# A sparse attention block on one core: the first tile's slot groups, the late neighbour lists and a late mean factor

## The chip, the cores and the metric

The kernel runs on 1 core of a Trainium2 chip, in one launch. The metric is the device time in microseconds (us). Time before: a median of 1792.07 us over 3 runs, from 1788.15 to 1799.92 us.

## The reference

One layer of graph attention over 4096 nodes with rows of 512 floats, float32 throughout, followed by a feed-forward block and a layer norm:

```
hs, ht = layer_norm(x), layer_norm(h_target)           # 4096 x 512
q, k, v = ht @ Wq + bq, hs @ Wk + bk, hs @ Wv + bv     # 8 heads of 64
logits = q.k / 8, -1e30 where adj == 0                 # 4096 x 4096, int32 adjacency
ctx = softmax(logits) @ v
ht = layer_norm(ht + ctx @ Wo + bo)
y = ht + gelu(ht @ W1) @ W2                            # W1 512 x 2048, W2 2048 x 512
out = layer_norm(x + y)
```

The adjacency is sparse: it is symmetric, has its diagonal set, and about 16 of 4096 entries of a row are ones (at most 39 here). So the kernel never forms the 4096 x 4096 logits: it makes lists of neighbours and gathers their key and value rows.

## The kernel before

**Two parts, written out by hand.** In part one, three generators are woven: `projections()` computes key and value rows of all nodes and writes them to a table `kvd` in device memory; `prepare()` makes the neighbour lists of tiles 0 to 15 (`NA` = 16, the early lists), sorts their rows by degree and starts the first query rows; `fill()` makes the lists of the next 7 tiles (`FILL` = 7). In part two, four generators are woven: `att` (attention), the chain of `feed(g)` (feed-forward), `other_lists()` (the last 9 tiles of lists, then `sort(1)` of tiles 16 to 31), and `weights()` (the second half of W1 and W2).

`_weave` keeps a due time for each generator and always runs the one that is due first; what a generator yields is added to its due time. These due times are units of the plan, not microseconds. Attention takes 60 units (`UNIT`) for a group of two tiles, and so does `feed`. `other_lists` starts at `WAIT` = 100 units and multiplies what `edges` yields by 2.2; a tile of late lists yields 12 in all, so that it takes 26.4 units. A stream that yields `None` sleeps until another one has run.

**Lists (`edges`, L716).** A tile of 128 adjacency rows comes in four quarters of 512 KB (`quarter`, L708, issued on SP). Those of tiles below `RINGED` = 22 go into rows 0 to 7 of a buffer `ring`; the later ones into two rows called `wide`. ScalarE takes the sign (L733), VectorE multiplies by positions (L740) and takes maxima (L742), and after four quarters decodes them (L749 to L766). Quarters are asked for ahead of the one in work, also by the last early tile for those of the first late tile.

**Sort (`sort`, L808).** Degrees are counted into bins with two matmuls and scans, ranks are computed (L864 to L867), and 16 indirect DMAs on GpSimd (POOL) scatter the records (L871), each 3.0 units after the last in part two. The records of part two must be there when attention asks for those of tile 16.

**Attention.** Tiles hold rows of like degree; tile i has a cap of neighbour slots. The order of caps by group is [11], [13, 14], [15, 15], [16, 17], [17, 18], [19, 19], [20, 22], [23, 24], [39, 12], [38, 13], [24, 14] and so on to [18]: 17 groups, 603 slots. Slots are worked in groups of `S` = 3 with what remains of the cap at the end. POOL gathers one slot (128 rows of 4 KB) with each L985. VectorE multiplies keys by the query (L1239) and sums per head (L1244), ScalarE takes the exponential (L1248, L1257) and scales the third slot (L1223), VectorE scales the first two (L1200) and adds some (L1204), TensorE adds the transposed values into `cps` (L1211). Gathers run 4 slot groups ahead (`AHEAD`) in `ring`, which has 17 rows for them at first and 20 once the lists are done; `place` says which rows.

**`finish` (L1096)** spreads the rest of a tile over later steps of attention (`advance()` runs every open tail twice per slot group): output projection (L1132), the copy of `h` (L1137), statistics (L697), variance plus epsilon (`n_ve`, L680), the power -1/2 on POOL (`power`, L687), the mean factor on VectorE (`negmean`, L692), the normalization on ScalarE (L1150), the transposes (L1159). Only then is `h2T` there, for which `feed(g)` sleeps.

**`feed(g)`** makes the hidden layer (L1344), its gelu (L1347) and the output (L1353); `end` (L1294) then spreads the last layer norm over the steps of the next `feed`: sum (L1300), squares (L1305), `n_ve` (L1309), power (L687), mean factor (L1314), normalization (L1317), scatter of the rows on POOL (L1321).

Of the kernel before, what the change touches and what calls it, by code (L numbers as in the profile page):

```python
# [443 lines left out]
def adj_resnorm_kernel(  # L444
# [38 lines left out]
    NT = N // P  # L483
# [4 lines left out]
    NQ = 4  # L488
# [7 lines left out]
    TILES = [t for g in groups for t in g]  # L496
# [4 lines left out]
    NA, NBT = len(CAPS_A), len(CAPS_B)  # L501
    PARTS = ((0, len(CAPS_A)), (len(CAPS_A), len(CAPS_B)))
    S = 3
# [29 lines left out]
    with tc.tile_pool(name="keep", bufs=1) as keep:  # L533
# [17 lines left out]
        with ExitStack() as late:  # L551
# [152 lines left out]
            adjs = []  # L704
            DEEP = 8
            FILL = 7
            RINGED = NA + FILL - 1
# [12 lines left out]
            def edges(i):  # L720

                part = 1 if i >= NA else 0
                rec = Rs[part][:, i - PARTS[part][0], :]
                cand = lp.tile([P, SEG, 8], U16, name="cand", bufs=2)
                for h in range(NQ):
                    n = i * NQ + h
                    while len(adjs) < min(n + 2, NT * NQ):
                        adjs.append(quarter(*divmod(len(adjs), NQ)))
                    a, adjs[n] = adjs[n], None

                    sg = turn_of("signs", signs)
                    with behind(newest if i >= NA else []):
                        nc.scalar.activation(sg, a, AF.Sign, accum_out=dpart[:, i, h:h + 1])  # L733
                    ahead = min(n + DEEP - 1, n + 3 + n // 2)
                    while len(adjs) < min(max(n + 3, min(ahead, RINGED * NQ)), NT * NQ):
                        adjs.append(quarter(*divmod(len(adjs), NQ)))
                    yield 0.0 if i < NA else 0.7 if i < NA + FILL else 1.0
                    wd = sg.bitcast(U16)
                    with behind(logits):
                        nc.vector.tensor_tensor(wd, wd, lio, ALU.mult)  # L740
                    for s, (w0, w1) in enumerate(SEGS):
                        maxima[:] = [nc.vector.max(cand[:, h * SQ + s, :], wd[:, w0:w1]).ins]  # L742
                    if h == 1:
                        keep_rest()
                    if h % 2 and moms:
                        moments(moms.pop(0))
                    yield 1.8 if i < NA else 0.7 if i < NA + FILL else 1.0
                dec = dec_w
                nc.vector.tensor_single_scalar(dec[:, 0], cand, 255, op=ALU.bitwise_and)  # L749
                nc.vector.tensor_single_scalar(dec[:, 1], cand, 8, op=ALU.logical_shift_right)  # L750
                gid = lp.tile([P, 2 * SEG, 8], F32, name="gid")
                dec = dec.rearrange("p b s e -> p (b s) e")
                off = segoff.rearrange("p b q s -> p (b q s)")
                nc.vector.scalar_tensor_tensor(gid, dec, 0.0,
                                               off.unsqueeze(2).to_broadcast([P, 2 * SEG, 8]),
                                               op0=ALU.is_gt, op1=ALU.mult)
                nc.vector.scalar_tensor_tensor(gid, dec, 2.0, gid, op0=ALU.mult, op1=ALU.add)
                flat = gid.rearrange("p s e -> p (s e)")
                for r in range(RE // 8):
                    top = rec[:, E0 + r * 8:E0 + (r + 1) * 8]  # L760
                    nc.vector.max(top, flat)
                    if r + 1 < RE // 8:
                        nc.vector.match_replace(flat, top, flat, 0.0)
                held.append((rest_d[i * P:(i + 1) * P, :], flat))
                has = lp.tile([P, MAXE], F32, name="ehas")
                nc.vector.tensor_scalar(has[:, :RE], rec[:, E0:E0 + RE], 0.0, 0.0, op0=ALU.is_gt,  # L766
                                        op1=ALU.add, accum_out=cnt[:, i:i + 1])
                yield 2.4 if NA <= i < NA + FILL else 4.0
# [45 lines left out]
            def sort(part):  # L814

                i0, n = PARTS[part]
# [52 lines left out]
                for i in range(n):  # L869
# [5 lines left out]

                    tc.declare_no_dep(ins.ins, group=f"scatter{part}", reason="other rows")
                    tc.add_to_no_dep_group(f"scatter{part}", ins.ins)
                    yield 3.0 if part else 1.3
                done.add(part)


# [119 lines left out]
            def front(i, idle=0):  # L1001
# [28 lines left out]
                for kc in range(KC):  # L1030
# [10 lines left out]

            SG = [(i, j0, min(S, cap - j0)) for i, (_, cap) in enumerate(TILES)
                  for j0 in range(0, cap, S)]
            kvs, rests, fronts = {}, {}, {}
            place = [11]
            for i, _, n in SG:
# [48 lines left out]
            def finish(i, p, cps, group, hs, mv):  # L1095
# [48 lines left out]
                ve = shifted(sp, mv[:, :nh, :], nh, "n2")  # L1144
                yield
                rs = power(sp, mv[:, :nh, :], nh, "n2", ve)
                yield
                nm = negmean(sp, mv[:, :nh, :], rs, nh, "n2")
                for j, h in enumerate(hs):
                    nc.scalar.activation(h, h, AF.Identity, bias=nm[:, j:j + 1], scale=rs[:, j:j + 1])  # L1150
# [144 lines left out]
            def end(group, xs, po):  # L1295
# [14 lines left out]
                yield  # L1310
                rs = power(sp, None, nt, "n3", ve)
                yield
                nm = sp.tile([P, nt], F32, name="n3_nm")
                nc.vector.tensor_mul(nm, sm[:, :nt, 0], rs)  # L1314
                yield
# [81 lines left out]
                for g in gens:  # L1397
                    yield from g

            WAIT = 100.0  # L1400
            AHEAD = 4
            ADDS = 11
            HEAVY = 30
# [67 lines left out]
                        load_quarter(pool, q + 2, nc.scalar)  # L1471

            def other_lists():
                for cost in ed:
                    yield 2.2 * cost
                keep_rest()
                yield from sort(1)

# [37 lines left out]
```

## Time and profile before

| | |
|---|---|
| median of 3 runs | 1792.07 us |
| the profiled execution | 1783.65 us, of which the span (first to last instruction) 1781.9 us |
| TensorE busy | 1666.0 us, 93% of the span |
| VectorE busy | 1425.0 us, 80% |
| ScalarE busy | 1240.4 us, 70% |
| POOL busy | 1018.9 us, 57% |
| mean granted TensorE clock | 0.971 |
| bytes moved | 461.0 MB, 259 GB/s over the span |

The profile gives each engine's busy time as an average over stages that have different limits, so that the views by time window and by waits matter more. A busy TensorE is not TensorE at its peak. On POOL the 0.3 us between two indirect DMAs are not counted as busy. The first list of part two is worked at 382.55 us of the span, its last at 708 us, the 16 scatters from 768.22 to 851.57 us.

### The profile page before, as it was taken

The page shows a single profiled execution, that of the slowest core. Times are in us where ns is not written, and L with a number is a line of the kernel's source. Part 1 is how long each engine was busy: PE and PEld are TensorE (multiplying, and loading weights), DVE is VectorE, ACT ScalarE, POOL GpSimd, SP SyncE. Part 2 cuts the span into 40 slices and gives each one's busy share as a digit, 9 for nine tenths or more (in the row PEclk, how much of TensorE's full clock was granted, in tenths as well). Part 3 has the DMA queues.
Part 4 walks back from the last instruction along what each step waited for, and adds up shares of the span by engine and source line. Part 5 has one row for each costly group of instructions (what it writes and reads, how often), then busy time and mean ns, then how long its engine had stood idle before and what let it go on. Part 6 is the DMA issues. An engine that isn't in the chain of part 4 may idle for free. (4 is left out here: it accounts for less than half of the span.)

```text
span 1781.9 us, 22463 instructions
## 1 busy us (share of the span) xinstructions
PE 1666.0 (93%) x6850; PEld 1078.9 (61%) x6850; DVE 1425.0 (80%) x2449; ACT 1240.4 (70%) x3133; POOL 1018.9 (57%) x822
## 2 busy tenths in 40 slices
PE   7999994889999999997989999999999999999997
PEld 3444443656666776665657667666666666666665
DVE  6887787868788989996989898989897888988500
ACT  5876673648777888675777877787776777877511
POOL 1000146655557566778886787777677767764101
PEclk9999997899999999998999999999999999999998
DMA  9999988877778797867888788877667777675000
GB/s 353 383 388 367 344 272 324 318 249 270 250 241 308 273 322 268 271 204 232 285 298 284 274 282 294 295 259 260 234 218 269 249 235 239 233 260 194 21 4 26
DMA packets 141610, 461.00 MB, mean 259 GB/s; under 512 B 18036, under 2 KB 23048, under 8 KB 141480
## 3 DMA queue, kind: packets, MB, share of 16 engines
q0 software_dynamic: 96272, 342.33, 56.7%
q1 hardware_dynamic: 37392, 94.06, 14.9%
q10 hardware_dynamic: 7816, 23.08, 3.3%
q8 instruction: 57, 0.93, 0.2%
q14 instruction: 73, 0.60, 0.1%
HBM read 430.61 MB, written 28.79 MB: 258 GB/s over the span
## 5 line engine op out<-in xcount | busy, mean ns | idle before, releaser
L985 POOL DMA_INDIRECT kv<-kvd,rec x603 | 795.4, 1319 | 335.4 <-issue 118.5
L1344 PE MATMUL pf<-h2T,w 128*128 128x256 f32 (+1 forms) x2176 | 474.5, 372 | 4.5 <-ACT h2T L1163 4.5
L1353 PE MATMUL po<-w,gt 128*128 128x512 f32 x1024 | 463.7, 594 | 0.0
L1344 PEld LDWEIGHTS pf<-h2T,w 128*128 128x128 f32 x2176 | 393.0, 193 | 74.3 <-issue 20.3
L1239 DVE TENSOR_TENSOR kv<-kv,tq 128x1536 f32<-128x1536 f32 (+2 forms) x211 | 351.1, 1675 | 55.6 <-DMA kv<-kvd,rec 52.0
L1223 ACT ACTIVATE kv<-kv,pa 128x64 f32<-128x64 f32 x1520 | 390.9, 336 | 4.4
L1244 DVE TENSOR_REDUCE lg<-kv 128x24 f32<-128x1536 f32 (+2 forms) x211 | 350.0, 1667 | 0.6
L1353 PEld LDWEIGHTS po<-w,gt 128*128 128x128 f32 x1024 | 187.6, 191 | 194.5 <-issue 193.1
L1211 PEld LDWEIGHTS cps<-ident,kv 128*128 128x128 f32 x1828 | 217.6, 144 | 121.5 <-issue 41.8
L1211 PE MATMUL cps<-ident,kv 128*128 128x128 f32 x1828 | 244.1, 280 | 50.1 <-DVE kv L1200 32.1
L1200 DVE TENSOR_TENSOR kv<-kv,p 128x1024 f32<-128x1024 f32 (+1 forms) x211 | 251.1, 1192 | 25.8 <-ACT p L1248 24.4
L687 POOL TENSOR_TENSOR n_rs<-n_ve,mhalf 128x2 f32<-128x2 f32 (+2 forms) x51 | 53.4, 1047 | 327.4 <-DVE n_ve L680 133.0
L733 ACT ACTIVATE kv<-kv 128x1024 uint8<-128x1024 int32 x128 | 134.4, 1052 | 53.4 <-DMA kv<-in_adj_dram 21.8
L1347 ACT ACTIVATE gt<-pf 128x512 f32<-128x512 f32 x128 | 76.4, 597 | 100.9 <-PE pf L1344 97.4
L1347 ACT ACT_TABLE_LOAD x110 | 141.1, 1283 | 1.8
L1132 PE MATMUL t<-wo,rb 128*128 128x512 f32 x256 | 121.0, 615 | 8.1 <-DVE rb L1122 8.1
L947 PE MATMUL pq<-wv,h2T 128*128 128x512 f32 x256 | 117.0, 600 | 3.3 <-DVE rbc L662 2.4
L947 PE MATMUL pq<-wk,h2T 128*128 128x512 f32 x256 | 119.1, 608 | 1.0 <-DVE h2T L928 1.0
L1031 PE MATMUL t<-wq,tq 128*128 128x512 f32 x256 | 116.8, 600 | 1.3 <-ACT tq L1024 1.3
L742 DVE MAX8 cand<-kv 128x8 uint16<-128x171 uint16 (+1 forms) x384 | 108.2, 324 | 1.2
L1248 ACT ACTIVATE p<-lg 128x24 f32<-128x24 f32 (+2 forms) x179 | 38.9, 218 | 75.3 <-DVE lg L1244 73.9
L947 PEld LDWEIGHTS pq<-wv,h2T 128*128 128x128 f32 x256 | 48.9, 193 | 66.8 <-issue 57.5
(163 smaller groups left out, 1586.0 us busy)
## 6 DMA issues: line engine op xcount, KB each, us to landing
kv<-in_adj_dram SPq DMA_DIRECT2D x128, 512.0 KB, 7.3
kvd<-tq ACTq DMA_DIRECT2D x23, 512.0 KB, 6.9
kv<-kvd,rec POOLq DMA_INDIRECT x603, 6.0
kv<-in_L_gnn_h_target_dram SPq DMA_DIRECT2D x32, 256.0 KB, 6.3
kv<-in_x_dram SPq DMA_DIRECT2D x15, 512.0 KB, 8.5
kvd<-kv ACTq DMA_DIRECT2D x9, 512.0 KB, 6.5
w<-in_L_gnn_W_dram SPq DMA_DIRECT2D x4, 1024.0 KB, 8.2
w<-in_L_gnn_W_dram ACTq DMA_DIRECT2D x4, 1024.0 KB, 14.1
```

What stands on the lines that cost most here:

```text
L733: nc.scalar.activation(sg, a, AF.Sign, accum_out=dpart[:, i, h:h + 1])
L947: nc.tensor.matmul(pkv, hT[:, kc, j * P:(j + 1) * P], w[:, kc, :], start=kc == 0, stop=kc == KC - 1)
L985: issues[:] = [nc.gpsimd.indirect_dma_start(out=dst, out_offset=None, in_=table[:, :], in_offset=bass.IndirectOffsetOnAxis(ap=idx, axis=0) ...
L1132: nc.tensor.matmul(pa, ct[:, c, :], wo[:, c, :], start=False, stop=c == KC - 1, skip_group_check=True)
L1200: nc.vector.tensor_tensor(v4, v4, p[:, j0:j0 + m, :].unsqueeze(3) .to_broadcast([P, m, H, HD]), ALU.mult)
L1211: nc.tensor.matmul(cps[:, c, :], kv[:, j, D + c * P:D + (c + 1) * P], ident, is_transpose=True, start=j0 + j == 0 and c == 0, stop=j0 + n ...
L1223: newest[:] = [nc.scalar.mul(v, v, pa[:, hd:hd + 1]).ins]
L1239: nc.vector.tensor_tensor(kv[:, :n, :D], kv[:, :n, :D], tq[:, :D].unsqueeze(1).to_broadcast([P, n, D]), ALU.mult)
L1244: logits[:] = [nc.vector.tensor_reduce(lg[:, :n, :], kv[:, :n, :D].rearrange("p j (h d) -> p j h d", h=H), AX.X, ALU.add).ins]
L1344: nc.tensor.matmul(pf[:, k, :], w1[(f0 + k) // KC][:, kc, (f0 + k) % KC * P:((f0 + k) % KC + 1) * P], h2T[:, kc, :w], start=kc == 0, stop= ...
L1347: nc.scalar.activation(gt, pf, AF.Gelu_apprx_tanh)
L1353: nc.tensor.matmul(po[j], gt[:, k, j * P:(j + 1) * P], w2[(f0 + k) // KC][:, (f0 + k) % KC, :], start=False, stop=f0 + k == FC - 1, skip_g ...
```

## The change

Six edits. The slot groups of tile 0 (11 slots) become 2, 3, 3, 3 instead of 3, 3, 3, 2. `edges` asks for no quarter beyond tile 22 while the early tiles run; `other_lists` asks for two itself and waits 6 units. `other_lists` starts at 134 units instead of 100 and multiplies by 1.6 (`PACE`) instead of 2.2. The scatters of `sort(1)` stand 4.5 units apart instead of 3.0. In `finish`, for tiles from 16 on, four yields instead of one stand between the power on POOL and the mean factor. In `end` two yields stand there instead of one.

```
@@ edges
+                    top = (NA + FILL if i < NA + FILL else NT) * NQ
-                    while len(adjs) < min(n + 2, NT * NQ):
+                    while len(adjs) < min(n + 2, top):
...
-                    while len(adjs) < min(max(n + 3, min(ahead, RINGED * NQ)), NT * NQ):
+                    while len(adjs) < min(max(n + 3, min(ahead, RINGED * NQ)), top):
@@ sort
-                    yield 3.0 if part else 1.3
+                    yield 4.5 if part else 1.3
@@ slot groups
             SG = [(i, j0, min(S, cap - j0)) for i, (_, cap) in enumerate(TILES)
                   for j0 in range(0, cap, S)]
+            short = TILES[0][1] % S
+            if short:
+                SG[:-(-TILES[0][1] // S)] = [(0, 0, short)] + [(0, j0, S) for j0 in
+                                                              range(short, TILES[0][1], S)]
@@ finish
                 rs = power(sp, mv[:, :nh, :], nh, "n2", ve)
-                yield
+                for _ in range(1 if i < NA else 4):
+                    yield
                 nm = negmean(sp, mv[:, :nh, :], rs, nh, "n2")
@@ end
                 rs = power(sp, None, nt, "n3", ve)
                 yield
+                yield
                 nm = sp.tile([P, nt], F32, name="n3_nm")
@@ constants
-            WAIT = 100.0
+            WAIT = 134.0
+            PACE = 1.6
@@ other_lists
+                for _ in range(2):
+                    adjs.append(quarter(*divmod(len(adjs), NQ)))
+                yield 6.0
                 for cost in ed:
-                    yield 2.2 * cost
+                    yield PACE * cost
                 keep_rest()
                 yield from sort(1)
```

## The prediction

> **What bounds the kernel now.** I read the busy times first, then windows of 10 and 50 us, then the timeline of TensorE for its gaps, and at each gap what the waiting engine waited for.
>
> ```profile
> PE 1666.0 (93%) x6850; PEld 1078.9 (61%) x6850; DVE 1425.0 (80%) x2449; ACT 1240.4 (70%) x3133; POOL 1018.9 (57%) x822
> ```
>
> TensorE (PE) is full nearly everywhere, and from 1650 us it works alone on the last feed-forward groups. The end comes when its work is done, so the kernel gains what PE stops losing. Its gaps of 0.8 us and more sum to 93.4 us: 14.2 in part one, 29.4 from 271 to 336 us, where part two fills, 49.8 later. The timeline shows the large later ones, by the instruction that ends each, with the idle time in brackets:
>
> ```profile
> 400.78 2.82 PE L1211 MATMUL cps<-ident,kv 128*128 128x128 f32 x12 [5.43 <-DVE kv L1200]
> 834.75 1.97 PE L1211 MATMUL cps<-ident,kv 128*128 128x128 f32 x8 [12.46 <-DVE kv L1204]
> 933.37 2.82 PE L1211 MATMUL cps<-ident,kv 128*128 128x128 f32 x12 [6.56 <-DVE kv L1200]
> 1257.78 1.11 PE L1159 MATMUL t<-ident,h 128*128 128x128 f32 x4 [4.06 <-DVE tq L1036]
> 1347.11 1.12 PE L1159 MATMUL t<-ident,h 128*128 128x128 f32 x4 [4.19 <-DVE tq L1036]
> ```
>
> Three causes. First, at 389 to 405 us: the feed-forward of group 0 is over, that of group 1 waits for its `h2T`, and just then the late lists start (first L733 at 382.55). Second, at 834 and 933: VectorE (DVE) waits for gathers, because POOL is full. In the windows the fifth pair is POOL; with 0.3 us between two instructions, 68.63 + 52 x 0.3 = 84.2 of 84 us:
>
> ```profile
> 768.00:852.00 84.00, 70.80 (x316) 50.15 (x315) 68.72 (x72) 58.25 (x161) 68.63 (x52) 0.92 0.69 217
> 852.00:950.00 98.00, 90.17 (x399) 61.36 (x398) 86.79 (x94) 71.48 (x204) 77.88 (x64) 0.97 0.87 297
> 823.03 1.76 DVE L1239 TENSOR_TENSOR kv<-kv,tq 128x1536 f32<-128x1536 f32 x1 [10.63 <-DMA kv<-kvd,rec]
> ```
>
> Third, at 1257 and 1347: DVE stands before the mean factor L692, since the power on POOL is queued behind gathers; behind L692 on DVE wait the values (L1204, L1200) and the query (L1036).
>
> ```profile
> 1246.75 0.16 DVE L692 SCALAR_TENSOR_TENSOR n_nm<-mv,n_rs 128x2 f32<-128x2 f32 x1 [4.10 <-POOL n_rs L687]
> 1339.84 0.16 DVE L692 SCALAR_TENSOR_TENSOR n_nm<-mv,n_rs 128x2 f32<-128x2 f32 x1 [7.84 <-POOL n_rs L687]
> ```
>
> **What the Trainium skill says.** "TensorE: Matmul & The Clock Gate", Part 1: an idle window of about 3.4 us halves the PE clock, and a busy one restores it. The trace agrees: after the gap at 834.75, 8 transposes take 1.97 us against 1.04 before it, and 16 L1344 take 5.18 against 3.62, so 2.5 us more are lost; after 400.78 it is 2.9 in the same way. The same page, Architectural detail, says that ScalarE, VectorE and POOL queues are strictly first in, first out; L692 above, with ready work behind it, agrees. "DMA: Bandwidth & Descriptors", Anatomy of one DMA, prices a POOL transfer at 2.0 us plus bytes at 436 GB/s, 3.2 us for 512 KB; here the median gather lands after 6.0 us, and I use the trace.
>
> **The change, part by part.** Sums stand against the profiled execution, 1783.65 us (span 1781.9), which is 8.4 below the median. A unit of the plan is about 1.49 us: from 100 units (382.55 us) to the first scatter at 358 units (768.22 us) pass 386 us.
>
> *Head: no late quarters early, and 2 slots first.* The first gather starts at 274.19:
>
> ```profile
> 274.19 0.97 POOL L985 DMA_INDIRECT kv<-kvd,rec  x1 [17.46 <-DMA rest_d<-gid]
> 282.32 1.76 DVE L1239 TENSOR_TENSOR kv<-kv,tq 128x1536 f32<-128x1536 f32 x1 [2.19 <-DMA kv<-kvd,rec]
> ```
>
> It needs the last `kvd` write, issued by ScalarE at 267.58. On SP two quarters, 1 MB, were issued at 265.42; at the 390 GB/s of this stage they hold the DMA engines for 2.7 us ahead of that write. Without them the first gather is up to 2.5 us earlier. The first L1239 waits for three gathers; with two it has its data one issue, 1.25 us, earlier. The sum of 3.7 is capped by the query: L1036 ends at 280.13, so L1239 moves at most from 282.32 to 280.13, by 2.2 us. Multiplications and reductions of the 11 slots are the same sum; a last group of three puts the 2.0 us of L1223 near the tile's end. The rows of `ring` begin 11, 13, 0, 3, 6 instead of 11, 14, 0, 3, 5, and for the next seven slot groups a row is reused after 5 groups instead of 6, so POOL may wait for the PE of the step just before. Bounds: 4 gained, 3 lost. I take 2 gained.
>
> *Late lists at 134 + 6 units instead of 100.* That is 40 x 1.49 = 60 us later, at about 442 us, past group 1. The gaps at 393.82, 400.78 and 405.19 are 1.98 + 5.43 + 1.59 = 9.0 us, with the clock 11.9. In that stretch DVE did 4.9 us of list work (four L740, twelve L742, first decodes) and waited 3.1 us for gathers beside four quarters. So `h2T` comes up to 8 us sooner; I take 6.5, as a boundary of groups isn't free of gaps even then. Upper end 12, lower end 0.
>
> *The same lists at 1.6 instead of 2.2.* Per tile DVE does four times (0.41 + 3 x 0.325) plus decodes of 3.2, some 8.7 us. In 26.4 units (39 us) that was 22% of DVE, in 19.2 units (28.6 us) it is 30%. From 500 to 750 us DVE was 90% busy (224.7 of 250), so it comes to 98% while the lists last; ScalarE (four times 1.24 us a tile) gets 5 points more on 82%. PE was full there (five windows miss 3.4 us of 250), and little slack remains at the boundaries of groups 2 to 4. No trace shows this load. Nothing lost at best; with attention's demand a few points higher in groups 4 and 5, up to 12 us. I take 4 lost, what one more gap with its cold clock costs.
>
> *Scatters 4.5 units apart.* `sort` begins at 134 + 6 + 9 x 12 x 1.6 = 312.8 units instead of 337.6; scatters run from 332.8 to 404.8 instead of 357.6 to 405.6. The end, which tile 16 waits for, stays. In the old stretch POOL loses 1.3 us per scatter every 5.2 us (25%), now about every 7 (18%). But no work leaves POOL, which never pauses from 768 to 958: what the stretch gains is the (357.6 - 332.8) / 4.5 = 5.5 scatters moved ahead of it, 7 us, and only as far as POOL was idle there (5.2 us beyond the 0.3s from 700 to 766). I take 5 gained, of the 19 of both gaps. Upper end 15, if evenly spaced gathers end the 12.46 us gap with its clock; lower end 0.
>
> *Mean factor three steps later from tile 16.* Waits before L692 go: 4.10, 7.84, 3.66, 5.30, 4.82 us (groups 10 to 14), 25.7 of DVE. In PE only two gaps answer to them, 4.06 + 4.19 = 8.25, and their clock, by the windows some 3: 11 gained. What is late instead is `h2T`, by three `advance()`, 1.5 slot groups. Each `feed` starts with its `h2T`, so once, near group 9, PE has 1.5 slot groups with no feed-forward: a slot group then takes DVE's 4.5 to 5 us, of which PE fills some 2: 4.5 lost. Net 6.5 gained; ends 12 gained and 3 lost.
>
> *One more yield in `end`.* L1314 waited 5.2 us in five places, three of them in the tail where PE alone works. The scatter of rows comes one step later and holds two `xt` buffers, which the next group asks for half a feed later. I take 0, from 2 gained to 2 lost.
>
> Sum: -2 - 6.5 + 4 - 5 - 6.5 = -16; with a share of the gap of 2.65 us at 1067 (same cause as 1257) -18. 1783.65 - 18 = 1765.7; from the median, 1792.07 - 18 = 1774.
>
> **The rivals.** *Gaps only trade places (0 to -8, about 1788).* A full PE in 412 to 750 us speaks for it: POOL is the pacemaker to 958, and an earlier start meets the same queue. Against it: the head and the gap at 400 lie where PE alone was starved, so they shift all that follows. *More goes than I count (-35, 1757).* If even spacing ends both POOL gaps (19 us and 5 of clock) with the L692 gaps, the sum is -16 - 19 = -35. For it: the gap at 834 is one wait of 10.63 us. Against: POOL's total work. *Slower: the denser lists overload DVE.* If the lists' 30% meets an attention that wants over 75% of DVE, as 99.5% in the window 700 to 750 hints, groups 3 to 5 become DVE-bound: if both together ask for 112 to 118% of the 9 x 28.6 = 257 us, PE starves for 31 to 46 us, less the 18 gained elsewhere: +13 to +28, or 1812. It decides from 107% on, where the excess eats the 18.
>
> **How the numbers follow.** My forecast, -8 to -28, gets 0.47; trading 0.19; more 0.17; slower 0.17. About 1% (18 us) is what a measurement of this kernel can tell from no change, and it halves my own case: faster 0.17 + 0.27 = 0.44; most of the slower case, 0.14, is over 1%; within 1% is the rest, 0.42. The likeliest time is 1774. Range 1752 to 1802: from -40 to +10, which leaves out most of the slower case and the end of the third.
>
> **What would show it.** Right: no list before 430 us, the gaps at 393 to 405 down to 3 us or less, first L1239 near 280, scatters from about 730 with POOL still without a pause to 950, L692 in groups 10 to 14 with waits under 1 us, and one new gap of PE of 3 to 5 us near 1160. Wrong: DVE at 98% and PE under 95% between 450 and 720; a gap over 10 us left at 830; `h2T` transposes that start new gaps at each boundary from group 9 on.

## The result, and the profile after

The changed kernel takes 1792.91 us in the median, the kernel before it 1789.51 us beside it: a ratio of 1.0022, 95% interval 1.0008 to 1.0036. The change costs some 4 us; the forecast was a gain of 18. (The ratio is not the quotient of the two medians, which is 1.0019. Here and below, microseconds that a version gains or costs are worked out from its ratio.)

The profiled execution of the changed kernel took 1796.3 us (span 1794.6), that of before 1783.65. This difference of 12.7 us isn't the size of the change: the first profile is at the low end of its kernel's runs (1782.41 to 1799.92), the second in the upper half of its own (1787.98 to 1802.88). Below, durations of waits are read from the profiles and the sizes of effects from the ratios.

Line numbers are those of each version's own file. In the changed kernel L1239 has become L1245, L1244 L1250, L1200 L1206, L1204 L1210, L1211 L1217, L1163 L1169, L1344 L1351, L1353 L1360 and L985 L986; L687 and L692 have kept their numbers. First, busy time by engine, and TensorE's gaps (in brackets the idle time ahead of the instruction and what ended it):

```profile
PE 1669.4 (93%) x6850; PEld 1077.6 (60%) x6850; DVE 1422.6 (79%) x2449; ACT 1232.2 (69%) x3127; POOL 1020.9 (57%) x822
```

```profile
404.91 0.47 PE L1217 MATMUL cps<-ident,kv 128*128 128x128 f32 x1 [4.52 <-DVE kv L1206]
663.65 1.11 PE L1022 MATMUL t<-ident,tq 128*128 128x128 f32 x4 [4.72 <-ACT rb L1124]
666.99 6.48 PE L1360 MATMUL po<-w,gt 128*128 128x512 f32 x8 [2.23 <-ACT gt L1354]
793.58 0.69 PE L1217 MATMUL cps<-ident,kv 128*128 128x128 f32 x2 [5.19 <-DVE kv L1210]
847.43 1.97 PE L1217 MATMUL cps<-ident,kv 128*128 128x128 f32 x8 [4.40 <-DVE kv L1210]
945.70 2.82 PE L1217 MATMUL cps<-ident,kv 128*128 128x128 f32 x12 [5.84 <-DVE kv L1206]
1091.26 4.21 PE L1351 MATMUL pf<-h2T,w 128*128 128x256 f32 x9 [6.13 <-ACT h2T L1169]
```

The gap of 12.46 us at 834 has become several of 3 to 5 us, the one at 1257 has gone, and those at 400 and 933 have stayed. New are 663 and 667, and 1091, where the feed-forward of a group waits for its `h2T`; in place of the gap at 1347 another such wait, of 3.03 us, stands at 1360. The new gap at 663 begins on POOL: a gather of `xt` waits for an earlier scatter into the output to land, the gathers of slots stand behind it in POOL's queue, and DVE waits for those. Timelines of POOL and of DVE:

```profile
646.99 0.97 POOL L986 DMA_INDIRECT xt<-in_x_dram,tags  x1 [7.16 <-DMA out_dram<-xt,tags]
```

```profile
658.61 1.76 DVE L1245 TENSOR_TENSOR kv<-kv,tq 128x1536 f32<-128x1536 f32 x1 [9.09 <-DMA kv<-kvd,rec]
```

The mean factor should have stopped waiting in groups 10 to 14. On DVE's timeline it stands in groups 10 to 12 like this ("issue": the profile shows no releaser):

```profile
1256.50 0.14 DVE L692 SCALAR_TENSOR_TENSOR n_nm<-mv,n_rs 128x2 f32<-128x2 f32 x1
1347.02 0.16 DVE L692 SCALAR_TENSOR_TENSOR n_nm<-mv,n_rs 128x2 f32<-128x2 f32 x1 [6.63 <-issue]
1431.77 0.16 DVE L692 SCALAR_TENSOR_TENSOR n_nm<-mv,n_rs 128x2 f32<-128x2 f32 x1 [7.36 <-POOL n_rs L687]
```

The wait of group 10 went, that of group 12 grew from 3.66 to 7.36. In groups 8 to 15 they sum to 26.6 us, against 26.9 before. The reason is in the order of instructions that the compiler emits. A yield sets only when the program, as it is traced, reaches an instruction; the place on the engine is the compiler's choice, and here it hardly follows the yields. DVE instructions between `n_ve` (L680) and L692, groups 9 to 15:

```
before            1  1  2  2  4  4  1
changed kernel    3  3  2  2  4  4  4
```

In groups 11 to 14 the two kernels have the same instructions there. What the three yields did move is `h2T`, and with it the start of each feed-forward.

The windows of the stretch in which POOL was full, and one of the stretch in which the lists are denser (busy us of PE, PEld, DVE, ACT, POOL, then granted clock, DMA share and GB/s):

```profile
500.00:700.00 200.00, 190.56 (x860) 132.26 (x859) 171.14 (x323) 163.61 (x399) 116.74 (x96) 0.97 0.79 277
768.00:852.00 84.00, 71.03 (x293) 48.96 (x292) 67.70 (x76) 52.94 (x140) 65.22 (x56) 0.93 0.78 253
852.00:950.00 98.00, 90.69 (x392) 61.63 (x392) 86.95 (x95) 73.16 (x203) 79.81 (x61) 0.96 0.83 281
```

From 768 to 852 TensorE has 71.03 us of work, as before (70.80): the long gap was cut into short ones and nothing was won. From 500 to 700 it has 190.56 instead of 197.62, with DVE at 171.14 us, no higher than before (174.96). So what was lost there wasn't DVE's capacity.

The late `h2T` shows at the end of the kernel. These are the last transposes of values and the last matmuls, first in the kernel before, then in the changed one:

```profile
1671.90 0.60 PE L1211 MATMUL cps<-ident,kv 128*128 128x128 f32 x4
1763.18 7.03 PE L1353 MATMUL po<-w,gt 128*128 128x512 f32 x16
```

```profile
1672.66 1.47 PE L1217 MATMUL cps<-ident,kv 128*128 128x128 f32 x12
1775.14 7.03 PE L1360 MATMUL po<-w,gt 128*128 128x512 f32 x16
```

From the end of the former to the end of the latter pass 97.7 us before and 108.0 us after. To the scatter of the last rows, which ends the work, it is 102.9 and 113.2 us; below, this time is called the tail.

### The profile page after: what moved, and what is told of

It reads as the page before. It is cut to its first block, busy times and chain, and to the rows that moved or that the text cites. A ratio compares the mean times of both kernels' runs of the same rounds, so it can differ in the third digit from the quotient of the medians.

```text
span 1794.6 us, 22449 instructions
## 1 busy us (share of the span) xinstructions
PE 1669.4 (93%) x6850; PEld 1077.6 (60%) x6850; DVE 1422.6 (79%) x2449; ACT 1232.2 (69%) x3127; POOL 1020.9 (57%) x822
## 5 line engine op out<-in xcount | busy, mean ns | idle before, releaser
L986 POOL DMA_INDIRECT kv<-kvd,rec x603 | 802.5, 1331 | 319.8 <-issue 128.8
L1351 PE MATMUL pf<-h2T,w 128*128 128x256 f32 (+1 forms) x2176 | 475.9, 372 | 13.0 <-ACT h2T L1169 11.5
L1360 PE MATMUL po<-w,gt 128*128 128x512 f32 x1024 | 465.2, 596 | 6.5 <-ACT gt L1354 6.5
L1351 PEld LDWEIGHTS pf<-h2T,w 128*128 128x128 f32 x2176 | 392.7, 193 | 81.1 <-issue 21.0
L1245 DVE TENSOR_TENSOR kv<-kv,tq 128x1536 f32<-128x1536 f32 (+2 forms) x211 | 351.3, 1675 | 57.9 <-DMA kv<-kvd,rec 52.5
L1250 DVE TENSOR_REDUCE lg<-kv 128x24 f32<-128x1536 f32 (+2 forms) x211 | 350.1, 1666 | 0.9 <-DVE R L762 0.2
L1360 PEld LDWEIGHTS po<-w,gt 128*128 128x128 f32 x1024 | 188.3, 191 | 200.7 <-issue 191.9
L1217 PE MATMUL cps<-ident,kv 128*128 128x128 f32 x1828 | 246.6, 280 | 48.0 <-DVE kv L1206 31.0
L1217 PEld LDWEIGHTS cps<-ident,kv 128*128 128x128 f32 x1828 | 217.2, 144 | 122.3 <-issue 40.4
L1206 DVE TENSOR_TENSOR kv<-kv,p 128x1024 f32<-128x1024 f32 (+1 forms) x211 | 251.3, 1192 | 18.7 <-ACT p L1254 13.8
L687 POOL TENSOR_TENSOR n_rs<-n_ve,mhalf 128x2 f32<-128x2 f32 (+2 forms) x51 | 46.1, 903 | 329.6 <-DVE n_ve L680 163.2
```

The costliest lines, as they stand in the source:

```text
L986: issues[:] = [nc.gpsimd.indirect_dma_start(out=dst, out_offset=None, in_=table[:, :], in_offset=bass.IndirectOffsetOnAxis(ap=idx, axis=0) ...
L1206: nc.vector.tensor_tensor(v4, v4, p[:, j0:j0 + m, :].unsqueeze(3) .to_broadcast([P, m, H, HD]), ALU.mult)
L1217: nc.tensor.matmul(cps[:, c, :], kv[:, j, D + c * P:D + (c + 1) * P], ident, is_transpose=True, start=j0 + j == 0 and c == 0, stop=j0 + n ...
L1245: nc.vector.tensor_tensor(kv[:, :n, :D], kv[:, :n, :D], tq[:, :D].unsqueeze(1).to_broadcast([P, n, D]), ALU.mult)
L1250: logits[:] = [nc.vector.tensor_reduce(lg[:, :n, :], kv[:, :n, :D].rearrange("p j (h d) -> p j h d", h=H), AX.X, ALU.add).ins]
L1351: nc.tensor.matmul(pf[:, k, :], w1[(f0 + k) // KC][:, kc, (f0 + k) % KC * P:((f0 + k) % KC + 1) * P], h2T[:, kc, :w], start=kc == 0, stop= ...
```

## The experiments

All ratios are against the kernel before, run beside the version on the same chip, with 95% intervals; a version has 2 to 22 runs. They were made on six chips, on which the kernel before had medians from 1784.9 to 1793.3 us, so only ratios are compared.

**One part at a time.** The short first slot group alone:

```
+            short = TILES[0][1] % S
+            if short:
+                SG[:-(-TILES[0][1] // S)] = [(0, 0, short)] + ...
```

> The kernel before with tile 0's slot groups as 2, 3, 3, 3 alone. Theory A (the head as in the prediction): the first multiplication waits for two gathers instead of three, 1 to 2 us gained. Rival (the query is what the first multiplication waits for next, and the last group of three costs it back): within 1 us, and DVE's first reduction chain ends no earlier.

Measured: 0.9969 (0.9956 to 0.9983), 5.5 us less. This part gains more than the 2 us that the prediction gave it.

The lists' part, `WAIT` 134, `PACE` 1.6 and scatters 4.5 units apart (without the edit of `edges` and the 6 units of waiting, which were not run by themselves):

> The kernel before with the late lists at 134 units and 1.6, and the scatters 4.5 apart, nothing else. Theory A (the prediction): 7 us gained at the boundary at 400 us and in the POOL stretch, net of the denser lists. Rival B (the denser lists take it back): 2 to 8 us slower, with new gaps of TensorE between 450 and 720 us. Rival C (gaps only trade places): within 2 us.

Measured: 1.0023 (1.0008 to 1.0039), 4 us more, in the range of rival B. TensorE's idle time (the brackets of its timeline, summed) rose by 9.5 us between 345 and 720 us (24.7 against 15.2) and fell by 4.6 between 720 and 860. The gap at the start of group 1 is there with no list near it:

```profile
399.06 1.53 PE L1211 MATMUL cps<-ident,kv 128*128 128x128 f32 x12 [2.04 <-DVE kv L1200]
406.14 2.25 PE L1159 MATMUL t<-ident,h 128*128 128x128 f32 x8 [5.55 <-ACT h L1150]
```

The mean factor alone (`for _ in range(1 if i < NA else 4): yield` ahead of `negmean`):

> The kernel before with four yields instead of one ahead of the mean factor from tile 16 on, nothing else. The order of VectorE's instructions that the compiler made has L692 one to three places behind n_ve in groups 9 to 14, as before, so the yields hardly move it. Theory D (the edit does not reach the instruction stream): the waits before L692 stay at 20 us or more in sum and the time is within 2 us. Theory A (the prediction): waits under 1 us each, 6 us faster.

Measured: 1.0072 (1.0044 to 1.0101), 13 us more. The waits before L692 sum to 25.1 us in groups 8 to 15. A new gap of 4.06 us at 1090 waits for `h2T`, and the tail is 113.2 us instead of 102.9: in the order of instructions, 246 matmuls follow the last transposes of values instead of 226. (A profile counts more: a product of two f32 tiles stands there twice, 16 records for the 8 of one step of L1344.)

The same yields, with the mean factor also bound to a place on DVE behind the newest logits:

```
+                with behind(logits if i >= NA else []):
                     nm = negmean(sp, mv[:, :nh, :], rs, nh, "n2")
```

> The kernel before with the four yields and the mean factor made to stand on VectorE behind the newest reduction of logits, from tile 16 on, so that it really is two slot groups later (8 to 16 instructions between n_ve and L692 in groups 9 to 14). Theory A: L692 waits under 3 us in sum, and the two gaps of TensorE at 1257 and 1347 us go, 6 to 11 us faster. Rival (h2T comes later, so each feed-forward starts later): new gaps of TensorE at the boundaries of groups 9 to 14, 0 to 10 us slower.

Measured: 1.0025 (1.0012 to 1.0038). Here the waits before L692 are gone (0.0 us in groups 8 to 15), but from 1000 to 1650 us TensorE is idle for 15.9 us, as before (16.6), and the tail stays at 113.2 us. The waits were removed together with a late `h2T`, and nothing came of it.

The density alone (`2.2 * cost` to `1.6 * cost`, start at 100 as before):

> The kernel before with only the density of the late lists changed, 1.6 instead of 2.2 units. Theory A (the density is what costs, as predicted): 3 to 6 us slower, 1.002 to 1.003, with TensorE's idle time between 345 and 720 us up by 4 to 9 us and DVE at 95% or more there. Theory B (the density is hidden, and the loss of the lists' part comes from moving the lists to where groups 3 to 5 are, with their scatters closer to the gathers): within 2 us of before.

Measured: 0.9997 (0.9975 to 1.0019). The ratio shows no cost of the density, though the profile has 21.1 us of idle TensorE from 345 to 720.

**The changed kernel without its mean edit and without the yield in `end`.**

> The changed kernel with the mean factor's three yields and the extra yield in end taken back; the short first slot group, the lists past group 1, their density and the scatters stay. Theory A (the mean edit costs: the feed-forward of every group starts 1.5 slot groups later, and the work that TensorE does alone at the end grows by 7.8 us): 4 to 9 us faster than the changed kernel, so 0.996 to 0.999 of the kernel before; from the h2T copy of group 16 to the end 71.8 us instead of 79.6; the gap of 6 us near 1091 us gone. Theory B (parts simply add): slots -5.5 and lists +4.1 give -1.4 us, 0.9992. Theory C (the loss lies in lists and scatters): as the changed kernel, 1.002.

Measured: 1.0007 (0.9992 to 1.0022). Slots and lists cancel each other. In this company the mean edit and the yield in `end` cost 0.15% together, 2.7 us, which the intervals don't tell from nothing; alone the mean edit cost 13.

**Which engine is the bound?** Three kernels leave work out. These three, and later the one with the reciprocal, also leave out the jump to the general path that the kernel takes for unusual inputs. The scatters of part two leave POOL:

```
+                    if part:
+                        ins = nc.sync.dma_start(recs_d[part][i * P:(i + 1) * P, :], R[:, i, :])
```

> The kernel before with the 16 scatters of part two left out of POOL: their rows go out in natural order from SP, so the neighbour lists of part two are not sorted into their tiles. Theory A (the gap at 834 us comes from POOL's total work, of which the scatters are 16 x 1.3 = 21 us): the gap of 12.5 us and the one of 6.6 us at 933 go, some 15 us off the total, 0.992. Theory B (gaps trade places, since other engines are full too): under 6 us off the total, 0.997 or more, with TensorE's idle time coming back after 860 us.

Measured: 0.9995 (0.9974 to 1.0015). With none of the 16 scatters on POOL, the gap before L1204 (here L1210) is still there with 7.63 us, and at 933 one of 1.45 us is left:

```profile
841.18 1.97 PE L1217 MATMUL cps<-ident,kv 128*128 128x128 f32 x8 [7.63 <-DVE kv L1210]
```

The total hasn't moved, but it doesn't measure the scatters alone. After all work, at the very end, an instruction of POOL of the kind DRAIN takes 8.3 us, where it takes 0.97 us in the kernel before and in each of the other versions. These are its three at that place, first in this version, then in the kernel before (ns, minimum, median and maximum):

```profile
L1517 POOLq DRAIN  x3: 44/107/8322, 1786.0 to 1794.8; - x3
```

```profile
L1511 POOLq DRAIN  x3: 44/107/972, 1780.1 to 1781.6; - x3
```

With 1.8 us more in the instruction ahead of it, 9 us come on at the end that no other version has. If every run of it has them, the scatters are worth some 10 us, and what their place costs stays open.

Half of the first feed-forward product left out in groups 8 to 14:

```
-                        for kc in range(KC):
+                        for kc in range(KC // 2 if 7 < g < 15 else KC):
```

> The kernel before with half of the first feed-forward product left out in groups 8 to 14: 7 x 64 matmuls of 0.232 us, 104 us less of TensorE's work, nearly all of it beside the attention after 1060 us. Theory A (attention is paced by another engine than TensorE, so a full TensorE is no bound): from the h2T of group 7 to the last transposes of values 704 us becomes 670 or more, and the total falls by under 40 us. Theory B (TensorE is the bound, as predicted): 610 to 630, the total 80 to 100 us less.

Measured: 0.9824 (0.9783 to 0.9864), 32 us less (2 runs). Half of the columns of the multiplication left out from tile 16 on:

```
+                            W = D if i < NA else D // 2
-                            nc.vector.tensor_tensor(kv[:, :n, :D], kv[:, :n, :D],
+                            nc.vector.tensor_tensor(kv[:, :n, :W], kv[:, :n, :W],
```

> The kernel before with half of the columns left out of the multiplication of keys and query from tile 16 on: some 80 x 0.88 = 70 us less of DVE's work, beside the attention after 1060 us. Theory A (DVE and what it waits for pace the attention): from the h2T of group 7 to the last transposes 704 us becomes 650 to 670, the total 30 to 55 us less. Theory B (TensorE is the bound): 695 or more, and under 10 us off the total.

Measured: 0.9986 (0.9965 to 1.0006), 2.5 us less. The windows from 1060 to 1650 us of the kernel before, of less TensorE and of less DVE, in this order, each from its own profile:

```profile
1060.00:1650.00 590.00, 573.71 (x2395) 382.33 (x2393) 511.32 (x581) 448.74 (x1173) 417.66 (x315) 0.98 0.74 248
```

```profile
1060.00:1650.00 590.00, 525.93 (x2072) 323.37 (x2071) 524.68 (x596) 462.11 (x1215) 434.86 (x322) 0.95 0.75 255
```

```profile
1060.00:1650.00 590.00, 571.77 (x2411) 381.30 (x2410) 445.52 (x577) 435.72 (x1154) 383.14 (x320) 0.99 0.74 252
```

Taking 70 us from DVE gives next to nothing, taking 104 from TensorE gives 32; what 21 us less of POOL give is hidden by the end of that version. By their own forecasts, less DVE work speaks against DVE as the pace of attention, and less TensorE work against a TensorE that bounds it alone: from the `h2T` of group 7 to the last transposes of values pass 673.2 us with less TensorE work and 699.6 with less DVE work, against 699.9 before. So TensorE is the bound, as the prediction read it, only by a small margin. In the kernel with less TensorE work TensorE is idle for 64.5 us from 1000 to 1650 us (16.6 before), and 42.7 of them (11.5 before) lie before the transposes of `h`: there the chain from a tile's attention to its `h` takes over, with the clock at 0.95. The start of a group then looks like this:

```profile
1341.12 0.47 PE L1159 MATMUL t<-ident,h 128*128 128x128 f32 x1 [7.81 <-ACT h L1150]
```

**When the feed-forward starts.** The opposite of what the mean edit does: `h2T` three steps sooner.

```
-                for _ in range(1 + 3 * slow):
+                for _ in range(1 + 3 * slow if i < NA else 1):
                     yield
                 pa = ps.tile([P, D], F32, name="t", bufs=2)
```

With the short first slot group:

> The kernel before with the short first slot group, and from tile 16 on the output projection of a tile one step after the rescaling instead of four: the opposite dose of the mean edit, h2T comes 1.5 slot groups sooner. Theory A: the work that TensorE does alone at the end shrinks by about half of what the mean edit added (8 matmuls fewer in the order of instructions after the last transposes of values, where the mean edit put 20 more), so 2 to 4 us less than 71.8 from group 16 to the end, and the total 2 to 5 us under the short slot group alone: 0.994 to 0.996. Theory D (it is the wait before the output projection that is needed): TensorE waits for rb or ct in every group, some 1 us a group, and the total is 5 to 10 us over the short slot group alone, 1.000 to 1.003.

Measured: 0.9916 (0.9894 to 0.9938), 15 us less. And this edit alone:

> The kernel before with only one edit: from tile 16 on the output projection comes one step after the rescaling instead of four. If the start of the feed-forward is the lever (three steps later cost 5 to 13 us): 3 to 10 us less than before, 0.994 to 0.998, from the last transposes to the end 96.8 us instead of 102.9. If the earlier result with the short first group owed its 0.992 to a meeting of the two edits: 0.998 to 1.002.

Measured: 0.9959 (0.9940 to 0.9978), 7.3 us less, with a tail of 96.8 us in both. But this edit changes a second thing: in both versions the waits before L692 in groups 8 to 15 fall to 12.5 us, from 26.9 before. Which of the two brings the gain isn't separated. A larger dose, all yields of this kind down to one and for early tiles too (the first seven had one already), with the short slot group:

> The kernel before with the short first slot group, and the yields between a tile's rescaling, output projection and h2T brought down to one each, from the first tile on: a larger dose against the mean edit (in the order of instructions 202 matmuls follow the last transposes of values, against 226 before, 218 with the smaller dose and 246 with the mean edit). Theory A (attention from the first gather to the last transposes takes the same time whatever feed-forward work lies beside it, and what is left after it adds to the end): from the last transposes to the end 88 to 92 us instead of 102.9, and 4 to 9 us under the smaller dose: 0.987 to 0.990. Theory D (the steps were needed as cover for rb and ct): TensorE stalls at L1117 and L1159, attention takes 10 us or more longer, and the total is 0.994 or more.

Measured: 1.0001 (0.9987 to 1.0015). The tail is only 91.2 us, but TensorE now waits before the output projections of tiles that had these steps as cover, 21.8 us in all against 6.0 with the smaller dose (timeline of TensorE):

```profile
742.23 6.03 PE L1136 MATMUL t<-wo,rb 128*128 128x512 f32 x8 [4.96 <-DVE rb L1126]
952.98 6.47 PE L1136 MATMUL t<-wo,rb 128*128 128x512 f32 x8 [6.37 <-DVE rb L1126]
```

Of the places tried, the one three steps sooner is the best; the mean edit moved the start to the other side.

**The changed kernel with its start restored.** The mean edit kept as it is, and the early projection added, so that 226 matmuls follow the last transposes, as before:

> The changed kernel as it is, with that same edit: the mean factor stays three steps late, the output projection comes three steps earlier, so the feed-forward of a group starts when it did before (226 matmuls after the last transposes, as before). If the late start of the feed-forward is what the mean edit costs: 3 to 8 us less than the changed kernel, 0.998 to 1.000 of the kernel before, from the last transposes to the end 102.9 us. If the cost lies in the mean factor's new place among DVE's instructions: as the changed kernel, 1.002 or more.

Measured: 0.9896 (0.9861 to 0.9931). Divided by the changed kernel's 1.0022 this is 0.987 (0.984 to 0.991, both intervals combined): 22 us, more than the 3 to 8 expected. Here the mean edit reaches DVE, presumably since its operands are ready sooner than the program comes to it:

```
DVE instructions between L680 and L692, groups 9 to 15
changed kernel                   3   3  2  2  4  4  4
with the early projection       10  10  8  5  8  3  8
```

The waits before L692 in groups 8 to 15 fall from 26.6 us to 3.1, the tail from 113.2 us to 102.9, and TensorE's idle time between 1000 and 1650 us from 18.5 to 6.8. The window of TensorE's fullest stretch:

```profile
1060.00:1650.00 590.00, 583.66 (x2475) 390.41 (x2473) 524.76 (x590) 455.00 (x1205) 429.31 (x317) 1.00 0.74 250
```

The same without lists, scatters and `end`:

> The short first slot group, the mean factor three steps late and the output projection three steps early, without the edits of the lists, the scatters and end. In the order of instructions DVE has 6 to 8 instructions between n_ve (L680) and the mean factor in groups 9 to 13, as against 2 to 4 in the changed kernel, so the waits before it are short. If the lists' part costs 4 us here too: 0.985 to 0.988. If it costs nothing in this company: as the changed kernel with the early projection, 0.990. If the mean edit brings nothing even where it reaches DVE: as slots and early projection alone, 0.992.

Measured: 0.9925 (0.9909 to 0.9941). Two things follow. The lists' part costs nothing in this company (0.9896 against 0.9925). And slots with the early projection had 0.9916 without any mean edit: even where it reaches DVE, the mean edit adds nothing that these runs can tell. It takes 6.7 us of waits (12.5 to 5.8 us in groups 8 to 15) and makes the tail 6 us longer.

**POOL's power out of the chain.**

```
-                rs = power(sp, mv[:, :nh, :], nh, "n2", ve)
+                rs = sp.tile([P, nh], F32, name="n2_rs")
+                nc.vector.reciprocal(rs, ve)
```

> The kernel before with the power of the second normalization replaced by a reciprocal on DVE (the square root is left out), so that the mean factor L692 never waits for POOL and nothing else moves. Theory B (these waits are not what TensorE loses; a full TensorE takes the time back elsewhere): L692 without waits, the total within 4 us of before. Theory P (as predicted, they cost TensorE some 11 us from group 10 on, and at the start of group 1 two more): 8 to 13 us less, 0.993 to 0.996, and the gaps of 4 us near 1257 and 1347 gone.

Measured: 0.9866 (0.9839 to 0.9894; 3 runs), 24 us less, where 8 to 13 were expected from the prediction's own reading. L692 no longer waits. That isn't all that moved: the time from `n_ve` to L692, which `h2T` waits out too, sums to 27.3 us over the 17 groups, against 66.0 before. Where L692 was forced behind the logits, its waits were gone as well and nothing was gained, so the 24 us can't be put down to DVE's waits alone. Of the gaps at 1257 and 1347 one of 2.7 us is left, and the start of group 1 has little from it, 7.2 us for 9.0 (lines of DVE, then of TensorE):

```profile
1238.46 0.15 DVE L692 SCALAR_TENSOR_TENSOR n_nm<-mv,n_rs 128x2 f32<-128x2 f32 x1
1321.85 0.14 DVE L692 SCALAR_TENSOR_TENSOR n_nm<-mv,n_rs 128x2 f32<-128x2 f32 x1
```

```profile
393.35 1.53 PE L1212 MATMUL cps<-ident,kv 128*128 128x128 f32 x12 [2.34 <-DVE kv L1201]
399.76 0.47 PE L1160 MATMUL t<-ident,h 128*128 128x128 f32 x1 [4.88 <-ACT h L1151]
```

Can a version with the square root keep this? Newton's method on DVE, 14 instructions in a chain, with the short first slot group:

```
+                nc.vector.tensor_scalar(rs, ve, 0.5, 0.5, op0=ALU.mult, op1=ALU.add)
+                nc.vector.reciprocal(rs, rs)
+                for _ in range(3):
+                    nc.vector.tensor_mul(sq, rs, rs)
+                    nc.vector.tensor_mul(sq, sq, ve)
+                    nc.vector.tensor_scalar(sq, sq, -0.5, 1.5, op0=ALU.mult, op1=ALU.add)
+                    nc.vector.tensor_mul(rs, rs, sq)
```

> The kernel before with the short first slot group, and the power of the second normalization worked out on DVE instead of POOL, square root included: a first value 2/(1+v), then three Newton steps, 14 small instructions a group, 17 groups x 14 x 0.16 = 38 us more on DVE. If DVE has that slack (70 us less of it gave 2.5): the gain of the reciprocal (-24) and of the slots (-5.5) less some 3, 0.984 to 0.988. If the longer chain from the statistics to h2T eats it: 0.992 or more.

Measured: 1.0017 (0.9997 to 1.0037). And in the changed kernel with the early projection:

> The changed kernel with the output projection one step after the rescaling from tile 16 on, and that same Newton on DVE. If the waits for POOL's power were all that is left to gain at the boundaries: 2 to 6 us under the version with the early projection alone, 0.986 to 0.989, and the gap of 5 us at the start of group 1 down to 3. If the waits are gone already in that version: the same as it, 0.990, or 3 us more for the longer chain.

Measured: 1.0028 (1.0013 to 1.0043), against 0.9896 with POOL's power. The timeline of DVE shows that 38 us was the wrong way to price it. In the chain each instruction needs the one ahead of it; they take 0.16 us each and start 0.2 us apart. Where all 14 stand together, in the first and in the last group, they take 2.7 us. In the other 15 groups DVE does other work between them, and from the first to the last of them pass 2.9 to 15.6 us in the first version, 3.5 to 23.6 in the second; all this time `h2T` waits. A part of such a chain, in the first version:

```profile
1272.28 0.16 DVE L696 TENSOR_TENSOR n_sq<-n_rs 128x2 f32<-128x2 f32 x1
1272.47 0.16 DVE L697 TENSOR_TENSOR n_sq<-n_sq,n_ve 128x2 f32<-128x2 f32 x1
1272.67 0.17 DVE L698 TENSOR_SCALAR n_sq<-n_sq 128x2 f32<-128x2 f32 x1
```

Two steps of three instructions, a chain of 8:

> The short first slot group and Newton on DVE as before, but two steps of three instructions, 8 instead of 14 in a chain: 1.6 us at each start of a group instead of 2.8. If the length of the chain at the boundary is what ate the gain of some 30 us (0.9866 x 0.9969 = 0.9835 without it, 1.0017 with 14): 8/14 of the way, 0.993. If a few instructions more on DVE anywhere cost so much through the order the compiler finds: no better than 1.000.

Measured: 0.9915 (0.9892 to 0.9938). The shorter chain, 1.5 to 10.8 us from first to last, brings 18 us back. That its length alone decides isn't shown, since the order of DVE's other instructions changes with it. Less work on DVE gave next to nothing, yet more of it at this one place ahead of `h2T` cost 9 us beside the slots and 24 beside the early projection. Two steps suffice only for variances near 1. For any variance, the fastest versions are the changed kernel with the early projection (0.9896), slots with the early projection (0.9916) and these two with the mean edit (0.9925); the runs don't tell them apart, and all three beat both kernels.

**Side by side.** Waits before L692 in groups 8 to 15, and the time from the last transposes of values to the last matmul, in us:

| version | ratio | waits | to the last matmul |
|---|---|---|---|
| before | 1 | 26.9 | 97.7 |
| changed | 1.0022 | 26.6 | 108.0 |
| changed, without mean edit and `end` | 1.0007 | 26.1 | 97.7 |
| mean edit alone | 1.0072 | 25.1 | 108.0 |
| mean edit, forced into place | 1.0025 | 0.0 | 108.0 |
| early projection alone | 0.9959 | 12.5 | 91.7 |
| slots, early projection | 0.9916 | 12.5 | 91.7 |
| slots, early projection, mean edit | 0.9925 | 5.8 | 97.7 |
| changed, early projection | 0.9896 | 3.1 | 97.7 |
| reciprocal | 0.9866 | 0.0 | 97.7 |

Every gain in this table goes with fewer waits. But with the mean edit forced into place the waits are gone and nothing is gained, and neither column alone gives the order of the ratios.

## Why the prediction was wrong

The sum was -18 us and the ratio says +4. The reading that TensorE is the bound held only in part: of 104 us taken from it, 32 came off the total. Two terms failed, of like size: the lists (-7.5 forecast, +4 measured alone) and the mean factor (-6.5 forecast; +2.7 measured in the changed kernel, together with `end`, and +13 alone). One term, the head, was too small.

*Head (-2).* Right in sign, too small: the short slot group alone gives 5.5 us. The other half of this term was void. On SP the last two quarters still go out at the end of part one (270.66 us after, 265.42 before), 94 in all before the first gather in both kernels, so the edit of `edges` didn't reach SP. (Its price didn't fit either: the window from 255 to 270 us shows 255 GB/s, not 390.) In the profile the first L1245 follows the first gather by 6.7 us (285.81 - 279.15) instead of 8.1. More lies at the start of group 1: from 25 us before its first transposes of `h` to 4 us after, TensorE's gaps sum to 5.5 to 6.9 us in every version with the short slot group and the power on POOL, and to 8.5 to 10.7 us in every one without the short slot group that keeps this power (10.4 in the kernel before). These 4 us are about what the term lacked.

*Lists, density and scatters (-6.5 + 4 - 5 = -7.5).* Measured alone: +4. The step that failed is the claim that the late lists delay the `h2T` of group 1. The first list does start late (424.00 us) and the scatters do start at 734.78, but the gap at the start of group 1 stays: 0.89 + 4.52 + 1.12 = 6.5 us after, and with the lists' part alone 2.37 + 2.04 + 5.55 + 1.02 = 11 us. So the lists were not its cause; what the changed kernel wins there comes with the short slot group. POOL's power has a small part in it (7.2 us with the reciprocal). The cause of the rest remains open. The density's cost of 4 isn't shown (-0.5 with an interval of 4 us to each side). Whether the scatters were worth 5 by their place isn't settled, since the version without them has 9 us of its own at the end. The reading that a full POOL makes the gaps at 834 and 933 fits 933, where 1.45 of 6.56 us are left without the scatters. At 834, 7.63 of 12.46 us stay, though POOL then has pauses of up to 2.8 us. The rival that gaps only trade places described this part best: the 12.46 us at 834 became 5.19, 3.38 and 4.40. Why the lists' part costs 4 us alone and nothing beside the early projection isn't settled. The wait of 7.16 us on POOL at 647 us can't be all of it: the changed kernel with the early projection, with the same lists and 22 us less, has it too, with 6.53 us at 643, and the lists alone, which cost 4 us, have none at that place.

*Mean factor (-11 + 4.5 = -6.5).* This step failed in both halves. The first was that three yields take L692 out of DVE's way; they moved it by no instruction in groups 11 to 14. That POOL's power in this chain costs something was right: without it the kernel gains 24 us. But that gain comes with an earlier `h2T`, and where the waits alone were removed, at the price of a later one, there was none. The second half, the late `h2T`, was priced as one gap of 4.5 us near group 9 and nothing at the end. The gap is there, 6.13 us at 1091, and a second one, 3.03 us at 1360. But the term left out is the tail: a feed-forward that starts 1.5 slot groups later leaves 20 more matmuls, 10.3 us, for the time when TensorE works alone. The tail holds no extra work, for both kernels have 6850 matmul records; it costs what the stretch before it doesn't give back. In the two profiles this stretch, from the first gather to the last transposes of values, became only 3.3 us shorter (1395.0 us for 1398.3), though 10.3 us of work had left it; profiles differ by as much from run to run. The ratios of the mean edit (+13 alone, +4.5 when forced into place) and of its opposite (-7.3 alone, -9.5 on top of the slots, -22 on top of the changed kernel) agree in sign. Their sizes do not: the tail is 10.3 us longer with the mean edit alone, forced into place or in the changed kernel alike, and 6.1 shorter with the early projection alone or beside the slots, so what differs lies beside attention. That remainder isn't explained.

*`end` (0).* Nothing shows a cost, though this yield was never run alone. Up to 1650 us the waits before L1314 grew from 2.7 to 15.1 us, but they grew to 11.1 with the mean edit alone, where `end` is as before.

Of the signs that were named, the scatters came as forecast, from 734.78 us. Near misses are the first list at 424.00 us (named was 430) and the new gap, 6.13 us at 1091 instead of 3 to 5 near 1160. The gaps at 393 to 405 down to 3 us, the first multiplication near 280 us (285.81), POOL without a pause (1.92 us at 831) and L692 under 1 us did not come. Of the signs against it, DVE at 98% didn't come (85.6% from 500 to 700), nor did a gap over 10 us at 834. Of the sums one doesn't come out: half of the chance 0.47 is 0.235, and 0.27 was taken.

## What to carry to other kernels

A yield, or any other change of the order in which a program is traced, is a request: before pricing what it hides, count in the emitted order how many instructions it puts ahead of the waiting one, for here the answer was none in four of the five groups that waited. When a step is moved later, follow it to the end of its chain and count what is left there when the other work is over; here it was 10.3 us. And a share of busy time doesn't say which engine can be loaded: 70 us taken from DVE gave next to nothing, while 14 small instructions ahead of `h2T` in each group cost 9 to 24 us. A version that leaves work out should be followed to its very last instruction before its total is believed.

## What was not expected of the hardware

Small dependent instructions on DVE (128x2) take 0.16 us each and start 0.2 us apart in a chain, so 14 of them take 2.7 us where nothing stands between. The same kernel before had a median of 1784.9 us on one chip and 1793.3 on another, a difference of 8.4 us and more than most effects measured here. In the version with 16 indirect DMAs fewer on POOL (717 instead of 733) its longest DRAIN at the end took 8.32 us, in the 19 other profiles 0.97. Within one profiled execution there is noise of the same size: the kernel with the mean edit alone has the same order of TensorE, DVE and ScalarE instructions as before up to the transposes for `h2T` of group 8, yet from the first gather to the normalization of group 7 it took 703.4 us against 694.1. A difference of 10 us between two profiles shows where waits are, not what they cost.
